# First layer of a two-layer graph network: gate products with one factor in PSUM, and the last bias added by a product with ones

## The chip, the cores and the metric

The kernel runs on one core of a Trainium2 chip. The metric is the device time of one execution, in microseconds (us), as the median of several runs. Engines are named as the profile names them: PE is the matrix engine (TensorE) and PEld its weight loads, DVE is VectorE, ACT is ScalarE, POOL is GpSimd, SP is SyncE, which here only issues DMAs. SBUF is the large on-chip memory; PSUM is the small one into which PE writes.

## The reference

There are 6250 nodes with 256 features, and 106250 edges sorted by target, among them one loop a node. The first layer runs a small network on the features at each edge's source (one of two, by the edge's kind), sums over a node's edges, and passes the sum through gates and three dense steps. The second layer is an attention layer. Both are added to their input and normalised.

```python
def layer0(feat, src, dst, rel, W_rel, b_rel, W_ih, b_ih, b_hh, W1, b1, W2, b2, W3, b3):
    S = feat[src]
    msgs = where(rel == r, relu(relu(S @ W_rel[r].T + b) @ W_rel[r].T + b), ...)   # r = 0, 1
    agg = segment_sum(msgs, dst)
    i, f, g, o = split(agg @ W_ih.T + b_ih + b_hh, 4, axis=-1)
    c = sigmoid(i) * tanh(g)
    hn = sigmoid(o) * tanh(c)
    x = relu(hn @ W1.T + b1)
    x = relu(x @ W2.T + b2)
    return x @ W3.T + b3

x = layernorm(x + layer0(x, src, dst, edge_type, ...))
x = layernorm(x + layer1(x, src, dst, ...))     # attention with 4 heads, softmax by target, layernorm, relu
```

## The kernel before

**Overall.** The messages depend only on the source node and the kind, so they are computed once for each node and kind and stored as a table in HBM (`parts0`). The first layer then gathers one row of that table an edge and sums the rows by target. The 100000 edges other than loops, sorted by target, are cut into 782 tiles of 128 edges. Fourteen tiles (two windows of seven) make a group, whose targets fill at most 128 node slots: there are 56 groups, numbered 0 to 55. The first layer ends with a table `rows1` in HBM, and the second layer gathers from it in the same way, tile by tile. A check takes this path, the function `fast`, when the edges are found sorted.

**The order.** Within `fast`, the order of each engine's instructions is the order in which the program writes them (`tc.manual_schedule()`): nothing is reordered afterwards, and an engine waits at its next instruction until its inputs and its buffer are there. The main loop of the first layer writes one gather (on POOL, an indirect DMA, L1367) and, four tiles behind it, one product of a one-hot matrix with the gathered rows (on PE, L1777, `sum0`). After each tile it calls `run.step()`, which goes through the chains that are under way. A chain is a Python generator; `yield n` means that its next piece is written n tiles later. After the last tile, `run.finish()` writes what is left of all chains, still in steps.

**The chains of the first layer.** `turn` takes a group's finished sum, adds the loops' share (L1549, twice) and transposes it (PE L1560, DVE copy L1563). `update` takes the groups together: four at a time up to group 47 (12 quads), then two pairs, and then groups 52 to 55 one by one, so 18 updates. An update with `cols` = 512, 256 or 128 columns goes through these steps, with pauses of `slow` tiles (3 early on, 1 in the last updates) between them:

1. for each half m = 0, 1: gates `gi`, `gg`, `go`, each of two products into one PSUM tile (L1627) and a sigmoid or tanh by ACT from there into SBUF (L1635); then `gg * gi` on DVE, in place, into the cell (L1640), written when all three gates of the half are written;
2. tanh of both cells on ACT, in place in SBUF (L1644), a pause, then tanh times `go` on DVE into `hn` (L1647), both halves together;
3. the product with W1 (L1651) and its relu (L1655), the product with W2 (L1658) and its relu (L1660);
4. right after that relu, `b3` added on DVE to the features `xn` of each group (L1663). `b3r` holds b3 in all 128 partitions, 256 numbers in each;
5. for each group, the product with W3 (L1672), the features added to it on DVE out of PSUM (L1674) and the statistics (L1676, L1677);
6. the square root on ACT (L1681), the reciprocal (L1683) and the normalisation (L1688) on DVE, transposes on PE (L1697), a copy by ACT (`fyT`, L1701), another bias (L1703);
7. the product with the second layer's weights (L1710), copies by ACT (L1716, L1717), stores of the rows by SP (L1723). The last group's rows are stored by an indirect DMA on POOL instead (L1725).

All products of `turn` and `update` share one ring of five PSUM tiles of a bank each (`fpg`). The sums have two further banks, and one bank holds constants of DVE and ACT (`bank`).

**The seam.** After the last tile of the first layer, POOL first issues 18 gathers of the second layer that depend only on rows stored by then (`gather_early`); then comes L1725, after it three more such gathers, and then the gathers of the second layer. Rows of the last three groups that such an early gather lacked are added later by PE (L1859).

Of the kernel before, what the change touches and what calls it, by code (L numbers as in the profile page):

```python
# [33 lines left out]
F32 = mybir.dt.float32  # L34
I32 = mybir.dt.int32
AF = mybir.ActivationFunctionType
# [6 lines left out]
P = 128  # L43
N = 6250
D = 256
# [662 lines left out]
def gnn_kernel(  # L708
# [572 lines left out]
    with tc.If(odd_v == 0) as cmp:  # L1281
        fast(
            tc, x, WihT, bih, bhh, W1T, b1, W2T, b2, W3T, b3, Wg, att_src, att_dst, bias, gamma,
            beta, out, parts0, rows1, slots, cuts, kept, iota_f, iota_p, ident, idx0, idx1,
            first, mark, slot, low_i, tail_i, tail_x, idx_e, own_n, srcs,
        )
# [8 lines left out]
def fast(  # L1295
# [40 lines left out]
    nc = tc.nc  # L1336

    def at(ap, offset, dims):
        return bass.AP(tensor=ap.tensor, offset=ap.offset + offset, ap=dims)

    def rows(ap, n):
        return at(ap, 0, [[0, P], [1, n]])
# [57 lines left out]
    everyone = slice(0, P)  # L1400
# [40 lines left out]
    def ring(pool, shape, dtype, name, n):  # L1441

        of = rings.setdefault((name, id(pool)), [[], 0])
        if len(of[0]) < n:
            of[0].append(pool.tile(shape, dtype, name=f"{name}_{len(of[0])}"))
        of[1] += 1
        return of[0][(of[1] - 1) % n]
# [19 lines left out]
    with (  # L1467
# [14 lines left out]
        W3T_s = l0w.tile([P, D], F32, name="fW3T")  # L1482
# [1 line left out]
        bh = l0w.tile([P, 8], F32, name="fbh")  # L1484
        b1c = l0w.tile([P, 1], F32, name="fb1c")
        b2c = l0w.tile([P, 1], F32, name="fb2c")
        b3r = l0w.tile([P, D], F32, name="fb3r")
        bias_r = l0w.tile([P, D], F32, name="fbias")
        with nc.allow_non_contiguous_dma(reason="bias vectors, one element a partition"):
            nc.sync.dma_start(bg, bih.rearrange("(m p) -> p m", p=P))  # L1490
            nc.sync.dma_start(bh, bhh.rearrange("(m p) -> p m", p=P))
            nc.sync.dma_start(b1c, b1.rearrange("(p o) -> p o", o=1))
            nc.sync.dma_start(b2c, b2.rearrange("(p o) -> p o", o=1))
        nc.sync.dma_start(b3r, rows(b3, D))
        nc.sync.dma_start(bias_r, rows(bias, D))
        nc.sync.dma_start(WihT_s, WihT.rearrange("(k p) f -> p k f", p=P))
        nc.sync.dma_start(W1T_s, W1T.rearrange("(k p) f -> p k f", p=P))
# [104 lines left out]
        def update(groups, aT):  # L1602
            slow = min(3, max(1, (NG - 4 - groups[0]) // 4))
            cols = len(groups) * P
            at_w = lows_of([w for g in groups for w in windows_of(g)])
            if groups == [NG - 1]:

                xn = [rows_x[NG - 1]]
                yield 2
            else:  # L1610
                xn = [ring(up, [P, D], F32, "fxn", 8) for g in groups]
# [3 lines left out]
            hn = ring(up, [P, 2, 4 * P], F32, "fhn", 2)  # L1615
            cells = []
            for m in range(2):
                gate = {}
                for name, part, func in (
                    ("gi", 0, AF.Sigmoid),  # L1620
                    ("gg", 2, AF.Tanh),
                    ("go", 3, AF.Sigmoid),
                ):
                    c = 2 * part + m
                    pg = ring(upp, [P, 4 * P], F32, "fpg", 5)
                    for k in range(2):
                        nc.tensor.matmul(  # L1627
                            pg[:, :cols],
                            WihT_s[:, k, c * P : (c + 1) * P],
                            aT[:, k, :cols],  # L1630
                            start=(k == 0),
                            stop=(k == 1),
                        )
                    gate[name] = ring(up, [P, 4 * P], F32, "f" + name, 2 if part == 0 else 4)
                    nc.scalar.activation(  # L1635
                        gate[name][:, :cols], pg[:, :cols], func, bias=bg[:, c : c + 1]
                    )
                    yield (slow + 1) // 2
                cell = gate["gg"][:, :cols]
                nc.vector.tensor_mul(cell, cell, gate["gi"][:, :cols])  # L1640
                cells.append((cell, gate["go"][:, :cols]))
            yield slow - 1
            for m, (cell, go) in enumerate(cells):
                nc.scalar.activation(cell, cell, AF.Tanh)  # L1644
            yield slow
            for m, (cell, go) in enumerate(cells):
                nc.vector.tensor_mul(hn[:, m, :cols], cell, go)  # L1647
            yield slow
            p1 = ring(upp, [P, 4 * P], F32, "fpg", 5)
            for k in range(2):  # L1650
# [7 lines left out]
            nc.tensor.matmul(p2[:, :cols], W2T_s, z1[:, :cols], start=True, stop=True)  # L1658
            z2 = ring(up, [P, 4 * P], F32, "fz", 3)
            nc.scalar.activation(z2[:, :cols], p2[:, :cols], AF.Relu, bias=b2c)  # L1660
            for i, g in enumerate(groups):
                u = everyone
                nc.vector.tensor_add(xn[i], xn[i], b3r)  # L1663
            yield slow
            mv = ring(up, [P, 4, 2], F32, "fmv", 3)
            rstd = ring(up, [P, 4], F32, "frstd", 3)
# [2 lines left out]
            for i, g in enumerate(groups):  # L1669
                u = everyone  # L1670
                p3 = ring(upp, [P, 4 * P], F32, "fpg", 5)[:, : 2 * P]
                nc.tensor.matmul(p3, z2[:, i * P : (i + 1) * P], W3T_s, start=True, stop=True)  # L1672
                y = keep3[i][u, 0, :]
                nc.vector.tensor_add(y, p3[u, :], xn[i])  # L1674
                st = ring(up, [P, nc.vector.BN_STATS_DIM], F32, "fst", 3)
                nc.vector.bn_stats(st[u, :], y)  # L1676
                nc.vector.bn_aggr(mv[u, i, :], st[u, :])  # L1677
                yield 1
# [6 lines left out]
            for i, g in enumerate(groups):  # L1685
                u = everyone
# [5 lines left out]
            for i, g in enumerate(groups):  # L1692
                u = everyone
# [12 lines left out]
            for i, g in enumerate(groups):  # L1706
                u = everyone
# [80 lines left out]
        for n in range(TC + LAG):  # L1788
            if n < TC:
                g, t = order[n]  # L1790
                k, turns = n % WT, n // WT // 10 % 2
                if k == 0:
# [3 lines left out]
                    m = min(WT, TC - n)  # L1796
# [15 lines left out]
            if n >= LAG:  # L1812
                g, t = order[n - LAG]
# [13 lines left out]
    with (  # L1827
# [285 lines left out]
        while t < TC + LAG or late or queue or run.chains:  # L2113
# [8 lines left out]
            if 0 <= k < TC:  # L2122
# [3 lines left out]
                g = w // 2  # L2126
# [87 lines left out]
```

## Time and profile before

| | |
|---|---|
| median of 3 runs | 2231.43 us (2231.18 to 2232.48) |
| profiled execution, its own time | 2231.32 us |
| its span | 2229.5 us |
| busy: PE, DVE, ACT, POOL | 1576.9, 1259.0, 506.4, 1527.2 us |
| the first layer's gathers | from 197 to 1186 us of the span |
| the second layer's gathers | from 1186 to 2178 us |

The span is the time between the first and the last record of the profile; 1.8 us of the execution's own time lie outside it. Times within the trace are us from the start of the span. A group of instructions is named by its line, engine and operation, what it writes and what it reads (buffer numbers left out), shapes as partitions x elements, and a count; behind the bar stand the busy time in us and the mean duration in ns, and behind a second bar the idle time of that engine before the group, with what ended it. In the timeline, the first two numbers of a line are start and duration, and the brackets at the end hold the engine's idle time ahead of it. A matmul of float32 numbers shows as two records.

### The profile page before, as it was taken

How to read it: one execution, taken by the hardware profiler on the slowest of the kernel's cores; microseconds unless marked ns; L12 is line 12 of the kernel's file. 1: busy time of each engine (PE TensorE's matmuls, PEld its weight loads, DVE VectorE, ACT ScalarE, POOL GpSimd, SP SyncE). 2: the span in 40 equal slices, each digit the busy share in tenths (PEclk: the TensorE clock that was granted, in tenths of full speed). 3: DMA queues.
4: the chain of work that ended last, by engine and by line, in shares of the span. 5: the costliest groups of instructions: out<-in, count | busy, mean ns of one | idle time of the engine just before them, and what ended most of it. 6: DMA issues, size and time to landing. Idle time of an engine off the chain costs nothing. (4 is left out here: it accounts for less than half of the span.)

```text
span 2229.5 us, 22334 instructions
## 1 busy us (share of the span) xinstructions
PE 1576.9 (71%) x5848; PEld 789.2 (35%) x5848; DVE 1259.0 (56%) x3374; ACT 506.4 (23%) x1526; POOL 1527.2 (68%) x1604
## 2 busy tenths in 40 slices
PE   8997788888888888888996754654545545454563
PEld 5664233333333333333453522322322223232331
DVE  7562134334333333333543688887777777777785
ACT  3332012221222212222343022212112111212121
POOL 1303777777777777777776777777777777777770
PEclk9998799899999899999997967766767677676776
DMA  5335435555455555554565556556555555555551
GB/s 165 131 103 155 130 114 172 165 153 149 147 171 165 146 151 155 170 168 134 178 175 162 150 145 165 156 145 165 148 153 156 144 159 143 164 155 145 156 151 38
DMA packets 163982, 334.33 MB, mean 150 GB/s; under 512 B 42538, under 2 KB 74398, under 8 KB 163845
## 3 DMA queue, kind: packets, MB, share of 16 engines
q0 software_dynamic: 75968, 208.00, 34.3%
q1 hardware_dynamic: 86085, 121.77, 17.3%
q10 hardware_dynamic: 1792, 3.05, 0.5%
q8 instruction: 48, 0.79, 0.1%
q14 instruction: 89, 0.73, 0.1%
HBM read 280.16 MB, written 52.53 MB: 149 GB/s over the span
## 5 line engine op out<-in xcount | busy, mean ns | idle before, releaser
L1367 POOL DMA_INDIRECT G<-parts,fidx x782 | 748.3, 957 | 330.5 <-issue 218.4
L1367 POOL DMA_INDIRECT G<-rows,fidx x761 | 727.4, 956 | 231.8 <-issue 214.2
L1777 PE MATMUL fps<-G,oh 128*64 128x257 f32 (+1 forms) x1674 | 528.1, 428 | 146.3 <-DMA G<-parts,fidx 129.5
L2101 PE MATMUL fps<-gw,oh 128*64 128x264 f32 (+1 forms) x1674 | 433.7, 463 | 246.3 <-DVE gw L1992 246.1
L2101 PEld LDWEIGHTS fps<-gw,oh 128*64 128x64 f32 (+1 forms) x1674 | 222.7, 164 | 411.9 <-DVE gw L1992 266.0
L1777 PEld LDWEIGHTS fps<-G,oh 128*64 128x64 f32 (+1 forms) x1674 | 193.6, 148 | 454.7 <-DMA G<-parts,fidx 237.2
L1992 DVE TENSOR_TENSOR gw<-G,bank 128x1792 f32<-128x1792 f32 (+1 forms) x167 | 248.9, 1490 | 62.4 <-ACT gw L1991 60.4
L1545 DVE TENSOR_SCALAR kind<-fps 128x1 f32<-128x1 f32 x112 | 12.5, 153 | 315.0 <-PE fps L1777 315.0
L1627 PE MATMUL fpg<-faT,fWihT 128*128 128x512 f32 (+2 forms) x432 | 170.9, 519 | 0.2 <-DVE faT L1563 0.2
L1452 DVE TENSOR_TENSOR oh<-bank,fslot 128x1024 f32<-128x1024 f32 x112 | 136.1, 1215 | 7.2 <-ACT bank L1971 7.2
L1940 PE MATMUL turn<-fident,e 128*120 128x128 f32 (+2 forms) x30 | 12.3, 412 | 155.3 <-ACT e L2136 155.3
L1242 PE MATMUL fpm<-fWrT,fhT 128*128 128x256 f32 x392 | 92.9, 392 | 5.3 <-DVE fms L1250 5.3
L1627 PEld LDWEIGHTS fpg<-faT,fWihT 128*128 128x128 f32 x432 | 70.9, 190 | 69.1 <-issue 59.4
L1738 DVE COPY nd<-hr 128x4 f32<-128x4 f32 x53 | 10.1, 190 | 149.7 <-ACT hr L1716 149.7
L1228 PE MATMUL fph<-fxc,fWrT 128*128 128x512 f32 (+1 forms) x208 | 88.8, 579 | 4.7 <-DMA fWrT<-in_WrT_dram 4.7
L2047 ACT ACTIVATE fy<-fy,frs 128x256 f32<-128x256 f32 x112 | 66.8, 596 | 86.9 <-DVE frs L2044 39.4
L2041 ACT ACTIVATE frs<-fmv,eps_c 128x1 f32<-128x1 f32 x112 | 32.9, 294 | 235.7 <-DVE gw L1986 152.7
L1242 PEld LDWEIGHTS fpm<-fWrT,fhT 128*128 128x128 f32 x392 | 75.6, 196 | 24.3 <-DVE fms L1250 9.1
L1710 PE MATMUL fpg<-Wx,fyT 128*128 128x264 f32 x224 | 74.2, 460 | 3.0 <-ACT fyT L1701 3.0
L944 POOL DMA_INDIRECT packed<-frame,place x21 | 20.9, 995 | 76.7 <-DVE frame L909 70.6
L1250 DVE TENSOR_TENSOR fms<-fpm,fbrr 128x512 f32<-128x512 f32 x49 | 33.6, 688 | 68.7 <-PE fpm L1242 62.8
L2144 ACT COPY e<-G 128x28 f32<-128x28 f32 x112 | 23.8, 213 | 183.8 <-DMA G<-rows,fidx 147.2
(253 smaller groups left out, 1863.4 us busy)
## 6 DMA issues: line engine op xcount, KB each, us to landing
kept<-keep SPq DMA_DIRECT2D x56, 384.0 KB
k<-kept SPq DMA_DIRECT2D x56, 384.0 KB
dB<-slots SPq DMA_DIRECT2D x112, 128.0 KB
loop<-parts SPq DMA_DIRECT2D x110, 128.0 KB
parts<-fms SPq DMA_DIRECT2D x49, 256.0 KB
G<-parts,fidx POOLq DMA_INDIRECT x782
G<-rows,fidx POOLq DMA_INDIRECT x761
fxn<-in_x_dram SPq DMA_DIRECT2D x110, 64.0 KB
```

Source lines behind the costliest of these rows:

```text
L1228: nc.tensor.matmul(ph[:, :cols], WrT_s[:, r, k, m * P : (m + 1) * P], xc[:, k, :cols], start=(k == 0), stop=(k == 1),)
L1242: made = nc.tensor.matmul(pm[:, r, :], hT[:, r, k, j * P : (j + 1) * P], WrT_s[:, r, k, :], start=(k == 0), stop=(k == 1),)
L1250: nc.vector.tensor_add(ms.rearrange("p r f -> p (r f)"), pm.rearrange("p r f -> p (r f)"), brr)
L1367: return nc.gpsimd.indirect_dma_start(out=to_tile, out_offset=None, in_=table, in_offset=bass.IndirectOffsetOnAxis(ap=idx, axis=0),)
L1452: nc.vector.tensor_tensor(to[:, :nj, :], iota_s[:, None, :].to_broadcast([P, nj, SLOTS]), of[:, :, None].to_broadcast([P, nj, SLOTS]), op= ...
L1627: nc.tensor.matmul(pg[:, :cols], WihT_s[:, k, c * P : (c + 1) * P], aT[:, k, :cols], start=(k == 0), stop=(k == 1),)
L1710: nc.tensor.matmul(ph[u, :], hs[i][:, k, u], Wx[:, k, :], start=(k == 0), stop=(k == 1))
L1777: nc.tensor.matmul(sums[g][to, :], ohj, got[t], start=begins, stop=ends)
L1992: nc.vector.tensor_mul(gw[:, :, :D].rearrange("p j (h f) -> p j h f", h=H), of[:, :n, :D].rearrange("p j (h f) -> p j h f", h=H), ex[:, o ...
L2041: nc.scalar.activation(r, mv[u, k, 1:2], AF.Ln, bias=eps_c[u])
L2047: nc.scalar.activation(y, y, AF.Identity, bias=m, scale=r)
L2101: nc.tensor.matmul(sums[g][to, :], ohj, gw, start=begins, stop=ends)
```

## The change

Three things change in `update`. In the gate `gg`, the tanh is written back into the PSUM tile from which it was read, and the cell is computed on DVE from that tile and `gi` right after it, ahead of the gate `go`. The tanh of the cell is written into a further PSUM tile of the ring `fpg`, and the product with `go` reads it there; the two halves now follow each other with a pause of `(slow + 1) // 2` tiles after each tanh, where before both tanh and then both products were written with a pause of `slow` between. And `b3` is no longer added to the features on DVE: a second product, of a row of 128 ones with the row b3, adds it to the PSUM sum of W3. For it `b3r` becomes one row, loaded by a smaller DMA, and a memset on DVE fills the row of ones.

```diff
-        b3r = l0w.tile([P, D], F32, name="fb3r")
+        b3r = l0w.tile([1, D], F32, name="fb3r")
+        one_r = l0w.tile([1, P], F32, name="one_r")
+        nc.vector.memset(one_r, 1.0)
...
-        nc.sync.dma_start(b3r, rows(b3, D))
+        nc.sync.dma_start(b3r, at(b3, 0, [[0, 1], [1, D]]))
...
-                    gate[name] = ring(up, [P, 4 * P], F32, "f" + name, 2 if part == 0 else 4)
+
+                    gate[name] = (
+                        pg
+                        if name == "gg"
+                        else ring(up, [P, 4 * P], F32, "f" + name, 2 if part == 0 else 4)
+                    )
                     nc.scalar.activation(
                         gate[name][:, :cols], pg[:, :cols], func, bias=bg[:, c : c + 1]
                     )
+                    if name == "gg":
+                        cell = ring(up, [P, 4 * P], F32, "fgg", 4)[:, :cols]
+                        nc.vector.tensor_mul(cell, pg[:, :cols], gate["gi"][:, :cols])
                     yield (slow + 1) // 2
-                cell = gate["gg"][:, :cols]
-                nc.vector.tensor_mul(cell, cell, gate["gi"][:, :cols])
                 cells.append((cell, gate["go"][:, :cols]))
             yield slow - 1
             for m, (cell, go) in enumerate(cells):
-                nc.scalar.activation(cell, cell, AF.Tanh)
-            yield slow
-            for m, (cell, go) in enumerate(cells):
-                nc.vector.tensor_mul(hn[:, m, :cols], cell, go)
+                pc = ring(upp, [P, 4 * P], F32, "fpg", 5)[:, :cols]
+                nc.scalar.activation(pc, cell, AF.Tanh)
+                yield (slow + 1) // 2
+                nc.vector.tensor_mul(hn[:, m, :cols], pc, go)
             yield slow
...
-            for i, g in enumerate(groups):
-                u = everyone
-                nc.vector.tensor_add(xn[i], xn[i], b3r)
             yield slow
...
-                nc.tensor.matmul(p3, z2[:, i * P : (i + 1) * P], W3T_s, start=True, stop=True)
+                nc.tensor.matmul(p3, z2[:, i * P : (i + 1) * P], W3T_s, start=True, stop=False)
+                nc.tensor.matmul(p3, one_r, b3r, start=False, stop=True)
```

## The prediction

> **What bounds the kernel now.** I read the page's busy times and slices first.
>
> ```profile
> PE 1576.9 (71%) x5848; PEld 789.2 (35%) x5848; DVE 1259.0 (56%) x3374; ACT 506.4 (23%) x1526; POOL 1527.2 (68%) x1604
> ...
> PE   8997788888888888888996754654545545454563
> ...
> POOL 1303777777777777777776777777777777777770
> ```
>
> By busy time PE leads, but its share falls by half in the second layer while nothing else slows. POOL stands at 7 from slice 5 to slice 39, but for one 6 in slice 22, where the two layers meet (1170 to 1226 us). Why 7 and not 9, the waits of POOL tell (who waited for what: total us, times, longest), and then its group of the first layer's gathers:
>
> ```profile
> POOL G L1367 <- issue: 437.4, 1436, 0.3
> POOL G L1367 <- ACT G L1798: 92.5, 1, 92.5
> ...
> POOL rows L1725 <- ACT keep L1717: 5.4, 1, 5.4
> ```
>
> ```profile
> L1367 POOL DMA_INDIRECT G<-parts,fidx x782 | 748.3, 957 | 330.5 <-issue 218.4 <-ACT G L1798 92.5 <-PE fps L1777 5.2
> ```
>
> A gather takes about 0.95 us and the next follows 0.30 us after its end, waiting for nothing: a chain of 1.25 us a tile. The 92.5 us are before the first gather. From 197 to 2178 us the only real wait is the 5.4 us at the seam, where L1725 needs the last group's rows. So the time is POOL's: work on PE, ACT or DVE counts only where it makes a gather longer or lengthens that seam.
>
> Some gathers are longer. The timeline of all engines around 565 us shows why:
>
> ```profile
> 565.44 0.69 DVE L1640 TENSOR_TENSOR fgg<-fgg,fgi 128x512 f32<-128x512 f32 x1 [2.64 <-ACT fgg L1635]
> 565.50 1.45 POOL L1367 DMA_INDIRECT G<-parts,fidx  x1 [0.30 <-issue]
> ...
> 567.25 0.94 POOL L1367 DMA_INDIRECT G<-parts,fidx  x1 [0.30 <-PE fpg L1627]
> ```
>
> L1640, with both factors in SBUF, began just ahead of the gather and ended at 566.13. The gather took 0.50 us more than 0.95, and the next began 1.75 us after it instead of 1.25. I went through all gathers from 197 to 1213 us: each lengthened one (over 0.02 us) but the first has a DVE instruction across its start, and its excess is that instruction's end less the gather's start less 0.13 us (here 0.63 - 0.13). By line: L1647 3.24 us (11 gathers), L1640 2.47 us (11), L1663 1.33 us (15), L1549 1.26 us, L1703 0.52 us, L1688 0.27 us; with the first gather's own 0.04 and traces, 9.2 us in all. The groups of DVE, shapes apart, in the same stretch:
>
> ```profile
> L1452 DVE TENSOR_TENSOR oh<-bank,fslot 128x1024 f32<-128x1024 f32 x56 | 67.8, 1211 | 0.0
> ...
> L1674 DVE TENSOR_TENSOR keep<-fpg,fxn 128x256 f32<-128x256 f32 x56 | 23.8, 424 | 30.4 <-PE fpg L1672 28.1
> ...
> L1663 DVE TENSOR_TENSOR fxn<-fxn,fb3r 128x256 f32<-128x256 f32 x56 | 20.2, 417 | 0.0
> L1640 DVE TENSOR_TENSOR fgg<-fgg,fgi 128x512 f32<-128x512 f32 x24 | 16.6, 692 | 41.9 <-ACT fgg L1635 39.3 <-issue 2.6
> L1647 DVE TENSOR_TENSOR fhn<-fgg,fgo 128x512 f32<-128x512 f32 x24 | 16.4, 687 | 3.4 <-ACT fgg L1644 2.4
> ```
>
> The first two rows are the control: one factor lies in PSUM (`bank`, `fpg`). L1452 covers a gather's start 53 times and L1674 8 times, and not one of those gathers is lengthened.
>
> [...]
>
> **The change, part by part.**
>
> *Stalls removed.* After the change L1640's product reads a PSUM tile and `gi`, L1647's a PSUM tile and `go`; L1663 is gone. By the control none can hold a gather: 2.47 + 3.24 + 1.33 = 7.04 us. Of this 0.21 us fall on early gathers after 1186 us, which end in a wait anyway. **Gain 6.8 us.** Bounds: L1549, L1703 and L1688 stay, with 2.05 us now. Their starts shift with the order; an instruction of length L at a random phase costs about (L - 0.13)² / 2.5 on average, 0.05 us for 0.48 us, so 56 of L1549's second form and 56 of L1703 and L1688 each could cost near 7 us. They follow PE and ACT, which follow the gathers, so I keep 2 us: -1 to +2 us.
>
> *DVE and ACT work.* 56 additions of 0.417 us (23 us) go; DVE is busy about a third of this stage, hence nothing. The products move from SBUF to PSUM: L1674 (PSUM, 424 ns) against L1663 (SBUF, 417) gives 7 ns each. ACT's work keeps its count. Memset and smaller DMA come around 200 us, ahead of no gather: nothing, within 0.2 us.
>
> *The product with ones.* 56 more products of 256 columns, two records each. L1672 is the nearest row (39.7 us for 112 records, 0.71 us a product); fewer rows need not make it faster, so 0.35 to 0.9 us. PE gains 40 us in a stage of 990 us in which it is busy 848 us. Its idle time, mostly waiting for gathered rows, hides them, except near the seam. POOL runs up to 70 tiles ahead of PE before the ring of gathered tiles stops it.
>
> *The ring `fpg`.* Two more tiles an update, and `gg`'s tile is held until DVE has read it. A tile is taken again five allocations later, over a tile's time away: nothing, up to 1 us at the seam.
>
> *Steps moved.* From the W1 product on, an update is written one tile (1.25 us) later, its row stores on SP and the stores of `kept` behind them too. The early gathers need group 52's stores; SP issued these by 1170 us and the first such gather comes at 1186: 16 us of cover. The cell's product, earlier on DVE, waits there for `gg` from ACT, as before (39.3 us idle ahead of L1640); behind it wait one-hots and sums' tails that PE has 70 tiles for. Nothing, 0 to 0.5 us.
>
> *The seam.* Here the cover is gone: L1725 waits for the last group's chain, and 5.35 us of it stand out behind the early gathers. The timelines of POOL, of ACT and of PE there:
>
> ```profile
> 1207.69 0.95 POOL L1367 DMA_INDIRECT G<-rows,idx_e  x1 [0.30 <-issue]
> 1213.99 1.00 POOL L1725 DMA_INDIRECT rows<-rows_l,tail_i  x1 [5.35 <-ACT keep L1717]
> ```
>
> ```profile
> 1197.31 1.28 ACT L1681 ACT_TABLE_LOAD   x1
> ...
> 1198.92 1.28 ACT L1635 ACT_TABLE_LOAD   x1
> ...
> 1200.60 1.28 ACT L1635 ACT_TABLE_LOAD   x1
> ```
>
> ```profile
> 1176.03 2.28 PE L1777 MATMUL fps<-G,oh 128*128 128x257 f32 x4 [3.33 <-DMA G<-parts,fidx]
> ```
>
> At 1176 PE last waits for rows; from there to the last group's sum (1191.4) it works without a gap, so what is added there delays the chain. I followed the yields by hand. The one-by-one updates need four steps where they had three, so group 53's W2 product (0.49 us) moves behind that wait, and its product with ones (0.71) is new: +1.2 us. After the last sum, group 54's W1 product comes behind a gate of group 55, and its ones product delays the later gates: about +1.4 us. Group 54's square root moves from between `gi` and `gg` of the second half to between `gg` and `go`: tanh no longer needs a load of its own, one of the three loads goes, -1.3 us. Group 55's own ones product: +0.7 us. Sum **+2.0 us**, bounds -0.5 (PE has slack) to +4 us (each step waits). Behind L1725 queue the last three early gathers and the whole second layer, so this counts in full.
>
> *Sum:* -6.8 + 2.0 = -4.8 us. The profiled execution's 2231.32 us (span 2229.5) becomes 2226.5; the median stands 0.1 us above it: **2226.6 us**.
>
> **Rivals.**
>
> 1. *Slower: PE becomes the bound before the seam.* From 1080 to 1190 us PE is idle only 8 us, 3.3 of them at 1176, and ten ones products (7 us) fall there. If the granted clock, at 0.93 to 1.0 there, drops by a tenth, PE's last 110 us last 11 us longer and the seam's stall grows from 5.35 to about 17 us: +11.5 - 6.8 = +4.7, 2236 us. It decides from a growth of the stall over 6.8 us; measurable slowing needs 11.3. Against it: PE caught up three times after 1150 us.
> 2. *The collisions move.* L1549, L1703 and L1688 fall on gathers near the random rate: +4 us, 2230.6 us. For it: every step after the gates shifts. Against it: the same offsets recur in quad after quad today.
> 3. *A free seam.* PE's idle time takes the products and the dropped table load shows: -0.7 us there, 2224 us.
> 4. *The change doesn't do what it says:* the stall comes from the write or from `gi` alone; no gain, +2.0, 2233.4 us. Against it: 61 controls.
>
> **How the numbers follow.** Main case 0.55, rivals 0.10, 0.15, 0.17, 0.03. A measurement here can tell about 0.2%, 4.5 us, so "faster" means under 2227.0. The main case (2223.5 to 2229.5) lies there in some 6 of 10, 0.34; rival 3 adds its 0.17: faster 0.51. Slower is rival 1 with its higher half and little else: 0.10. Same 0.39. Range: the gain with a free seam and 1 us fewer collisions, 2222.8, to all but the worst of rival 2, 2231.0.
>
> **What would show it.** Gathers of 1.0 us and more under the gate products gone, the first layer's last gather near 1179 instead of 1186 us, L1452 and L1549 unchanged; two table loads, not three, in the last updates; a wait of some 7 us ahead of L1725. It is wrong if gathers are still lengthened under products with a PSUM factor, or if the wait ahead of L1725 passes 10 us.

## The result and the profile after

In runs of both kernels side by side the kernel after takes 2228.02 us (median; 2226.2 to 2233.2) and the kernel before 2233.26 us: a ratio of **0.9979, 95% interval 0.9971 to 0.9987**. In a second set of runs the medians are 2224.25 and 2228.55 us, the ratio 0.9982 (0.9975 to 0.9990). So the change is worth 4.3 to 5.2 us, against a forecast of 4.8. (The 2226.6 us of the forecast were reckoned from 2231.4 us; in the first of these sets the kernel before took 1.8 us more than that.)

Busy time and slices of the kernel after:

```profile
PE 1601.2 (72%) x5960; PEld 805.4 (36%) x5960; DVE 1235.8 (56%) x3319; ACT 504.7 (23%) x1526; POOL 1523.6 (68%) x1604
...
PE   8997789888888889989996754554555545455563
...
POOL 1303777777777777777776777777777777777770
```

PE gained 24 us net in its records, DVE lost 23, and slice 22 of POOL is still a 6. The waits of POOL (total us, times, longest), and its group of the first layer's gathers:

```profile
POOL G L1367 <- ACT G L1804: 90.8, 1, 90.8
```

```profile
POOL rows L1731 <- ACT keep L1723: 4.8, 1, 4.8
```

```profile
L1367 POOL DMA_INDIRECT G<-parts,fidx x782 | 744.2, 952 | 328.9 <-issue 216.4
```

The same three lines as before, little changed: the waits are 90.8 and 4.8 us where they were 92.5 and 5.4, and the mean gather of the first layer is 952 ns instead of 957. The groups of DVE in that stage, shapes apart (lines have moved: L1640 is now L1647, L1647 is L1655, L1674 is L1680):

```profile
L1452 DVE TENSOR_TENSOR oh<-bank,fslot 128x1024 f32<-128x1024 f32 x56 | 67.8, 1210 | 0.0
...
L1680 DVE TENSOR_TENSOR keep<-fpg,fxn 128x256 f32<-128x256 f32 x56 | 23.8, 425 | 73.1 <-PE fpg L1678 71.7 <-DMA loop<-parts 1.4
...
L1647 DVE TENSOR_TENSOR fgg<-fpg,fgi 128x512 f32<-128x512 f32 x24 | 16.6, 692 | 106.2 <-ACT fpg L1642 106.2
L1655 DVE TENSOR_TENSOR fhn<-fpg,fgo 128x512 f32<-128x512 f32 x24 | 15.3, 681 | 1.3 <-ACT fpg L1653 1.3
```

The gate products last as long as they did (692 and 681 ns), but one factor is now `fpg`, and **not one gather is lengthened under them any more**. The excess (what the gathers take over 0.95 us each, added up as in the prediction, here up to the last gather of the first layer) fell from 8.8 to 2.8 us; what is left is L1551 (the former L1549) 1.8 us, L1709 (L1703) 0.6, L1694 (L1688) 0.3. That is 6.0 us; in a second profiled execution of the kernel after it is 2.0, a fall of 6.8.

The seam is best read as three stretches. "Sum" is the start of L1545 (now L1547) on the last group, the first instruction that reads its sum:

| us | first to last gather of layer 1 | last gather to sum | sum to tail store | first gather to tail store |
|---|---|---|---|---|
| before | 987.8 | 6.7 | 22.6 | 1017.1 |
| after | 983.8 | 5.4 | 23.2 | 1012.3 |
| after, second profile | 980.9 | 8.7 | 23.8 | 1013.3 |

The tail store is L1725 (now L1731). From the first gather to it both profiles of the kernel after have about the forecast's gain (-4.8 and -3.8 us), divided up differently. From the tail store to the end, where no code was changed, the three profiles take 1015.6, 1017.8 and 1013.0 us: single executions scatter there by about as much as the change is worth.

The first two profiles can't be compared gather by gather without one more reading. The median distance from one gather to the next is 1251 ns before and 1254 ns after, in both layers, stalls or none. Over the 782 gathers of the first layer that is some 2 us against the kernel after: of the 6.0 us of stalls saved there, 4.0 are left in the first column. So the exact 4.8 us of this profile are in part chance. The experiments below show that the spacing is not a property of this kernel.

### The profile page after: what moved, and what is told of

The parts are those of the page before. It is cut to its first block, busy times and chain, and to the rows that moved or that the text cites. A ratio compares the mean times of both kernels' runs of the same rounds, so it can differ in the third digit from the quotient of the medians.

```text
span 2225.4 us, 22485 instructions
## 1 busy us (share of the span) xinstructions
PE 1601.2 (72%) x5960; PEld 805.4 (36%) x5960; DVE 1235.8 (56%) x3319; ACT 504.7 (23%) x1526; POOL 1523.6 (68%) x1604
## 3 DMA queue, kind: packets, MB, share of 16 engines
q1 hardware_dynamic: 85943, 121.64, 17.6%
## 5 line engine op out<-in xcount | busy, mean ns | idle before, releaser
L1783 PE MATMUL fps<-G,oh 128*64 128x257 f32 (+1 forms) x1674 | 510.9, 426 | 120.1 <-DMA G<-parts,fidx 100.1
L1547 DVE TENSOR_SCALAR kind<-fps 128x1 f32<-128x1 f32 x112 | 12.4, 152 | 177.5 <-PE fps L1783 177.5
L1647 DVE TENSOR_TENSOR fgg<-fpg,fgi 128x512 f32<-128x512 f32 (+2 forms) x36 | 20.6, 573 | 143.2 <-ACT fpg L1642 143.2
L1565 DVE COPY faT<-fpg 128x256 f32<-128x256 f32 x56 | 23.8, 425 | 97.5 <-PE fpg L1562 95.8
L1716 PE MATMUL fpg<-Wx,fyT 128*128 128x264 f32 x224 | 76.6, 472 | 1.3 <-ACT fyT L1707 1.3
```

What stands on the lines that cost most here:

```text
L1565: nc.vector.tensor_copy(aT[:, :, i * P : (i + 1) * P], pt.rearrange("p (k n) -> p k n", k=2))
L1716: nc.tensor.matmul(ph[u, :], hs[i][:, k, u], Wx[:, k, :], start=(k == 0), stop=(k == 1))
L1783: nc.tensor.matmul(sums[g][to, :], ohj, got[t], start=begins, stop=ends)
```

## The experiments

The first four (of the fourth, its first run) ran on a chip where the kernel before itself takes 3078 us. POOL waits there for other engines, in experiment 1's profile 526 us for L1992 on DVE in the second layer (2.7 us in the kernel before as profiled above), and PE's mean granted clock is 0.72 instead of 0.83; why was not found. Of those four I use how long gathers were. Their times are given, but the ratios follow neither the stalls nor the products with ones: experiments 1 and 3 both have these products, and stand at 1.0083 and 0.9987.

The "port theory" of three expectations is a name only, for what the first of them puts in brackets: that a product with both factors in SBUF holds up a gather that starts under it. By what means it does so no run shows.

**1. One part alone: b3 by a product with ones, gates as before** (edit against the kernel before).

```diff
-                nc.vector.tensor_add(xn[i], xn[i], b3r)
...
+                nc.tensor.matmul(p3, one_r, b3r, start=False, stop=True)
```

> The kernel before with only the last part of the change: b3 added by the product with ones, no addition on VectorE; the gate products stay in SBUF. Port theory (a product with both factors in SBUF holds up a gather that starts under it; placement alone decides): the first layer's gathers lose only the share of the additions, their excess over 0.95 us falls from 8.8 to about 7.5 us (6.5 to 8.5), all of it under L1640, L1647 and L1549. Seam: if the products with ones lengthen the chain as predicted, from the last gathered tile to the tail store 29.3 us become 30.7 (29.3 + 0.7 for group 53 + 0.7 for group 55); if keeping the matrix engine busy saves it the slow clock after its wait, they become 28 or less. Time: -1 us by the port theory with a long seam, -3 with a short one. Rival (load theory: fewer VectorE instructions in all are what helps): excess falls by the share of VectorE time removed, 20 of about 360 us, so by 0.5 us.

Measured: excess 7.35 us, 5.3 of it under the two gate products, none under the addition that is gone. Ratio 1.0083 (1.0053 to 1.0113), where a gain of 1 to 3 us had been expected. The stalls of the gates don't depend on b3's path.

**2. The other part alone: gates in PSUM, b3 on VectorE** (edit against the kernel after).

```diff
+                nc.vector.tensor_add(xn[i], xn[i], b3r)
...
-                nc.tensor.matmul(p3, one_r, b3r, start=False, stop=True)
```

> The changed kernel with b3 added on VectorE again and no product with ones; only the gate products have a factor in PSUM. Port theory: excess of the first layer's gathers 2.8 + 1.3 = about 4 us (3.2 to 5.5), none of it under the two gate products, about 1.3 us under the addition of b3. Load theory: VectorE has the same work as before, so excess near 8.8 us. Seam: with no product with ones the matrix engine should wait before the seam and run slowly after it, as in the kernel before: 29 us or more from the last gathered tile to the tail store; if the product with ones only costs, 27.5 us. Time against before: -4.5 us by the port theory, 0 by the load theory.

Measured: excess 4.08 us, none under the gate products, 1.6 under b3's addition; ratio 0.9967 (0.9950 to 0.9983).

**3. The order of the change without PSUM.** Here the products come in the new places and with the new pauses, but both factors lie in SBUF (edit against the kernel after).

```diff
-                    gate[name] = (pg if name == "gg" else ring(...))
+                    gate[name] = ring(up, [P, 4 * P], F32, "f" + name, 2 if part == 0 else 4)
...
-                        nc.vector.tensor_mul(cell, pg[:, :cols], gate["gi"][:, :cols])
+                        nc.vector.tensor_mul(cell, cell, gate["gi"][:, :cols])
...
-                pc = ring(upp, [P, 4 * P], F32, "fpg", 5)[:, :cols]
+                pc = cell
```

> The changed kernel in its order, instruction for instruction, but with both factors of the gate products in SBUF again (tanh of the gate and of the cell written to SBUF, in place in the cell). Port theory: the gathers under these two products are held up again, excess 2.8 + about 5.7 = 8.5 us (5 to 11, as their phase against the gathers is another one), each excess equal to the product's end less the gather's start less 0.13 us. Order theory (the gain comes from writing the products at other places, or in two halves): excess stays near 2.8 us and the time equals that of the changed kernel. Time against before: 0 to +2 us less the share of b3, so about -1 (port), -4.7 (order).

Measured: ratio 0.9987 (0.9970 to 1.0005); excess 11.5 us, 8.7 of it under the gate products: somewhat above the upper end of the range, and four times what a theory of order allows. **So the place of one factor decides, not the order and not DVE's load.** With the control of 1 and 2 this is shown, not argued.

**4. A product of zeros added to the kernel before.**

```diff
-                nc.tensor.matmul(p3, z2[:, i * P : (i + 1) * P], W3T_s, start=True, stop=True)
+                nc.tensor.matmul(p3, z2[:, i * P : (i + 1) * P], W3T_s, start=True, stop=False)
+                nc.tensor.matmul(p3, toward[0:1, 1, :], b3r[0:1, :], start=False, stop=True)
```

> The kernel before with one more product of a single row added to each sum of W3, a row of zeros as weights, so that nothing is added to the sum: the matrix engine's work of the change without its other parts. Excess of the gathers: 8.8 us, unchanged within 1.5 us. Cost theory (as predicted: each product with ones in the seam's chain counts): from the last gathered tile to the tail store 29.3 becomes 30.7 us, time +1.4 us. Clock theory (the matrix engine waited 3.3 us at 1172 to 1176 us and then ran at half clock for 4 us; more work there keeps it from waiting): 27.5 to 28.5 us, no wait over 2 us before the seam, granted clock 1.00 in the ten us after it, time -1 us.

Measured on the first chip: excess 8.8 us, unchanged; ratio 1.0057 (1.0036 to 1.0078); the seam, with a wait of 32 us there, told nothing. It was run again where the kernel before takes 2227.4 us:

> The kernel before with one product of a row of zeros added to every output product of the first layer: 56 times 2 products become two, some 0.71 us each, and nothing else changes (the row of toward that it uses is zero by construction, b3 is still added on VectorE). Clock theory of the last groups: the 3.3 us that PE waited for rows and the half clock after it are filled, and from the last gather of the first layer to the tail store it takes 27.5 to 28.5 us instead of 29.3; the excess of the gathers stays at 8.8 us, so the time falls by about 1 us (0 to 2). Cost theory, as predicted: the product of the last group lies on the path, 29.9 to 30.9 us, and the time rises by 0.5 to 1.5 us. PE as bound: a wait over 6 us ahead of the tail store and a time 5 us or more longer.

Measured: 2229.23 us, ratio 1.0006 (0.9998 to 1.0014), 1.9 us above the kernel before and so a little more than the cost theory's 1.5; excess 8.1 us; 30.75 us from the last gather to the tail store: the cost theory's number, but not by its way. The last gather to the sum takes 5.6 us, 1.1 less than before in spite of the added products, as the clock theory has it (no wait for rows after 1051 us, and a granted clock of 1.00 from there to the sum); from the sum to the tail store it takes 25.2 instead of 22.6. There the two products of zeros on the path show, and one of them runs at half speed:

```profile
1190.89 0.69 PE L1673 MATMUL fpg<-fb3r,toward 1*128 1x256 f32 x2
...
1203.11 1.22 PE L1672 MATMUL fpg<-fW3T,fz 128*128 128x256 f32 x2 [0.46 <-ACT fz L1660]
1204.27 1.22 PE L1673 MATMUL fpg<-fb3r,toward 1*128 1x256 f32 x2
```

The first takes 0.62 us from start to start, the second 1.22. With what the half-speed W3 product takes more (1.22 against 0.70 us before) that is 2.4 of the 2.6 us. Neither theory alone was right.

**5. The kernel after again, beside the gates alone.** The second profiled execution and the second set of times told of above:

> The kernel after, unchanged, a second profiled execution beside the other kernels of this set. If the median period of the gathers (1254 ns in its first profile, 1251 in that of the kernel before) belongs to the kernel, it is 1254 again and the time stays where it was; if it is a matter of the single execution, it can be 1251, and the span is then 4 us shorter. Excess of the first layer's gathers 2.8 us again; 28.5 us from the last gather to the tail store if the full clock of the first profile is the kernel's, 29.5 or more if it was the execution's. Ratio to the kernel before 0.997 to 0.9987.

Measured: gathers 1251 ns apart. So the 1254 don't belong to the kernel (experiment 8's kernel, too, shows 1251 in one profile and 1254 in the next, though on another chip). The chip alone does not decide it either: on the chip of the first experiments, experiment 2 shows 1251 and the other three 1254. The excess is 2.0 us and the gathers' stretch 7.0 us shorter than before: **the gain of 6.8 us is there in full**. But the tail store starts 1013.3 us after the first gather, no earlier than in the first profile, although the last gather started 3 us sooner: the seam took 32.5 us, not 28.5. The gates alone on the same chip:

> The kernel after with b3 added to the features on VectorE as in the kernel before (no product with ones): the PSUM part of the change alone. By the prediction's steps the stalls under the gate products go (5.7 us), those under the addition of b3 stay (1.1 to 1.6 us), and the ones products' 1.4 us at the end are saved: ratio 0.9965 to 0.998, within 0.1% of the kernel after. If the ones products cost more than their own place at the end (PE late over the whole layer), gates alone is faster than the kernel after by over 2 us (ratio 0.9955 to 0.997).

Measured: 2222.91 us, ratio 0.9971 (0.9961 to 0.9982), in the mean 1.3 us below the kernel after (95% interval 0.2 to 2.3), less than the 2 us that the second theory asked for; excess 4.1 us, of which 2.1 under b3's addition. The change's second part takes 2.1 us of stalls away and is still no gain: in the profiles the tail store comes 1012.8 us after the first gather with the gates alone, and 1013.3 in the kernel after beside it. When PE last waited for gathered rows points to the reason (timelines of PE: gates alone, then the kernel after in both profiles):

```profile
1169.53 1.49 PE L1783 MATMUL fps<-G,oh 128*128 128x257 f32 x4 [3.11 <-DMA G<-parts,fidx]
```

```profile
1043.24 0.62 PE L1783 MATMUL fps<-G,oh 128*64 128x257 f32 x2 [0.34 <-DMA G<-parts,fidx]
```

```profile
1040.22 3.23 PE L1783 MATMUL fps<-G,oh 128*64 128x257 f32 x6 [1.28 <-DMA G<-parts,fidx]
```

In the kernel before this was 1176 us, as the prediction showed. With the ones products PE catches up with the gathers for the last time at 1040 to 1043 us and then runs behind them for 140 us to the sum. From there on a shorter gather no longer brings the sum forward. The products of zeros alone do the same to the kernel before: in experiment 4's second run PE last waited for rows at 1050 us.

**6. Four products where the change has one.** Three more products of zeros an output, all after the ones product, with no effect on the sums:

```diff
-                nc.tensor.matmul(p3, one_r, b3r, start=False, stop=True)
+                nc.tensor.matmul(p3, one_r, b3r, start=False, stop=False)
+                for more in range(3):
+                    nc.tensor.matmul(p3, toward[0:1, 1, :], b3r, start=False, stop=(more == 2))
```

> The kernel after with three more products of a row of zeros for every output product, all adding nothing to the sums: TensorE gets 168 products in two parts, 0.71 us each, some 120 us more. TensorE as the coming bound (rival 1): its waits in the first layer are used up, the ring of gathered rows fills, POOL waits, and the wait ahead of the tail store and before it adds up to 15 to 35 us, time 10 to 30 us above the kernel after. If TensorE has room: only the seam's share, 3 times 0.7 to 1.4 us, 2 to 6 us.

Measured: 2263.02 us, ratio 1.0155 (1.0141 to 1.0168), 38.8 us above the kernel after: PE as bound, and past my upper end. The gathers' excess is 1.6 us, so it is not they; POOL waits in two places (timeline of POOL):

```profile
1184.77 0.95 POOL L1367 DMA_INDIRECT loop<-parts,tail_x  x1 [24.18 <-DVE agg L1551]
...
1244.46 1.00 POOL L1733 DMA_INDIRECT rows<-rows_l,tail_i  x1 [17.56 <-ACT keep L1725]
```

24.2 us ahead of the last group's loop rows, whose tile is free only when an earlier group is through, and 17.6 at the tail store. The rows of the two kinds of products, and busy time and clock by stage (the column after POOL's is PE's granted clock):

```profile
L1680 PE MATMUL fpg<-fb3r,toward 1*128 1x256 f32 x336 | 129.0, 540 | 0.0
...
L1678 PE MATMUL fpg<-fb3r,one_r 1*128 1x256 f32 x112 | 55.0, 582 | 0.0
```

```profile
200.00:600.00 400.00, 373.10 (x1149) 175.35 (x1150) 122.83 (x379) 72.90 (x180) 302.63 (x320) 0.85 0.54 155
600.00:1000.00 400.00, 393.83 (x1264) 194.56 (x1263) 141.31 (x473) 92.42 (x242) 302.75 (x320) 0.87 0.55 158
1000.00:1170.00 170.00, 168.91 (x543) 88.95 (x541) 58.87 (x201) 41.27 (x109) 121.61 (x129) 0.83 0.54 156
```

```profile
200.00:600.00 400.00, 343.09 (x1056) 139.68 (x1056) 127.22 (x390) 73.29 (x182) 302.76 (x319) 0.90 0.53 154
600.00:1000.00 400.00, 351.45 (x1122) 147.95 (x1121) 138.67 (x464) 92.14 (x240) 302.95 (x319) 0.94 0.55 160
1000.00:1170.00 170.00, 160.78 (x586) 79.19 (x585) 69.66 (x249) 58.12 (x149) 128.71 (x135) 0.96 0.56 163
```

The second fence is the kernel after. 129 us of products were added. PE's busy time from 1000 to 1170 us was 160.8 of 170 already; with more of it (168.9) the granted clock was 0.83 there instead of 0.96, the same products took longer (the ones product 582 ns a record instead of 436), and the rest came out at the end. PE had not paused before it slowed: it has no wait from 1100 to 1142 us, and in that time a ones product takes 0.69 us at 1121.89 and the next 1.22 at 1125.87; without a wait again, 0.69 at 1159.50 and 1.22 at 1163.55. I had not put a falling clock into this expectation.

**7. More factors in PSUM.** In `turn` the first addition writes back into the sums, so the second has a factor there; in the second layer the sum, its scaling and an addition do the same.

```diff
-            for r, of in ((0, ps[:, :D]), (1, agg)):
-                nc.vector.scalar_tensor_tensor(agg, loop0[g][...], kind[:, r : r + 1], of, ...)
+            for r, to in ((0, ps[:, :D]), (1, agg)):
+                nc.vector.scalar_tensor_tensor(to, loop0[g][...], kind[:, r : r + 1], ps[:, :D], ...)
...
-            nc.vector.tensor_add(y, y, ps[u, :D])
-            read.add(g)
+            nc.vector.tensor_add(ps[u, :D], y, ps[u, :D])
...
-            nc.vector.tensor_mul(heads(y), heads(y), den...)
-            nc.vector.tensor_add(y, y, k3[u, 1, :])
+            nc.vector.tensor_mul(heads(ps[u, :D]), heads(ps[u, :D]), den...)
+            nc.vector.tensor_add(y, ps[u, :D], k3[u, 1, :])
+            read.add(g)
```

> The kernel after, in which three more operations of VectorE get one factor in PSUM: the first of the two additions of the loop rows in turn writes its result back over the sums in PSUM, so the second reads it there, and in the second layer's finish the sum, its scaling by 1/den and the addition of k3 keep their running value in PSUM, the sums being given free after the last of them. Placement theory: of the excess of the first layer's gathers the 1.8 us under the loop addition go, 1.0 stay; of the second layer's 6.6 us the 1.6 and 0.4 under the scaling and the addition go; with 7 ns for each operand in PSUM hidden, the time falls by 3 to 4 us against the kernel after, about 8 us against the kernel before (ratio 0.996 to 0.9975). Rival, the sums held longer delay PE: gathers of the second layer are unchanged but PE's wait for the free sums grows, and the time stays within 1 us of the kernel after (ratio 0.9975 to 0.999) or rises.

Measured: the first layer's excess is 0.6 us, nothing under the loop addition. Yet the ratio is 0.9986 (0.9979 to 0.9992), no better than the kernel after's 0.9982 on another chip. The last gather to the sum takes 8.4 us. This is the rival's ratio, though for another reason than it named: PE is behind since 1039 us, as in the kernel after since 1040. From there to the sum PE was without work for 4.2 us, in the kernel after's second profile for 3.8, and from the tail store to the end it takes 1014.4 us, where the kernel after takes 1017.8 and 1013.0. So no cost of the sums held longer shows.

**8. The same without the ones product**, b3 being added to the third product where it lies in PSUM:

```diff
-                nc.tensor.matmul(p3, one_r, b3r, start=False, stop=True)
+                nc.vector.tensor_add(p3, p3, b3r)
```

> The kernel e7 (loop rows and the second layer's sum kept in PSUM as well) with the ones product taken out and b3 added on VectorE to the third product in PSUM, so that this addition has one factor in PSUM: 112 products of some 0.36 us each leave TensorE, 56 additions of 0.42 us return to VectorE. If TensorE is late by then (e7 took 8.3 us from the last gather to the end of the last group's sum where the kernel after took 5.3), that stretch is 5.3 to 7 us here and the time 2 to 4 us below e7's 2223.9 (ratio to the kernel before 0.9965 to 0.998); if TensorE is not late, it is within 1 us of e7 (0.998 to 0.999). Excess of the first layer's gathers 0.6 us in both cases.

Measured: 2221.58 us, ratio 0.9966 (0.9953 to 0.9978), in the mean 3.0 us below the kernel after beside it (95% interval 1.3 to 4.7). The excess is 1.3 us, not 0.6, nearly all of it under L1692 and L1707 (formerly L1688 and L1703) and none under b3's addition. The last gather to the sum takes 7.5 us, though: a little over the expected end, and in this profile PE last waited for rows at 1042 us even so. Its clock is low there (a mean of 0.66 from 1040 to 1050 us, and 0.83 from 1140 to 1150; behind the wait, four records of L1714 take 2.13 us at 1044.58, and 1.16 at 1051.70), which may be why; no run tests it. Run again on another chip:

> The kernel e8, unchanged, once more: ratio to the kernel before 0.9955 to 0.9978, and first gather to tail store 1010 to 1011.5 us again, with 30 to 31.5 us from the last gather of the first layer to the tail store. If its lead over the kernel after was chance, the ratio is 0.998 to 0.999.

Measured: 2222.20 us beside 2231.03 for the kernel before, ratio 0.9958 (0.9944 to 0.9971). Excess 1.7 us. First gather to tail store 1010.8 and 1010.1 us in the two. In the second, with gathers 1254 ns apart, PE waits for rows up to 1174 us and the seam takes 27.6 us, less than expected. The addition of b3, and the tail store of that profile:

```profile
L1676 DVE TENSOR_TENSOR fpg<-fpg,fb3r 128x256 f32<-128x256 f32 x56 | 23.6, 422 | 33.1 <-PE fpg L1675 33.0
```

```profile
1203.91 1.00 POOL L1729 DMA_INDIRECT rows<-rows_l,tail_i  x1 [4.14 <-ACT keep L1721]
```

422 ns an addition where the product took 0.71 us of PE, and a wait of 4.1 us ahead of the tail store instead of the 8.8 of the kernel after's second profile. This version beats the kernel before in two sets, and the kernel after in the one set where both ran.

**9. The change with only its second part done so** (the edit of experiment 8, on the kernel after).

> The kernel after with only its second part done otherwise: the ones product is taken out, and b3 is added on VectorE to the third product where it lies in PSUM, so that the addition has one factor in PSUM and one in SBUF. 112 products (40 us) leave TensorE, 56 additions of 0.42 us return to VectorE; no gather should wait under the addition (2.1 us in the kernel with the gates alone). Theory, TensorE is late at the end of the first layer and the ones products are a part of that: first gather to tail store 1010.5 to 1012, time 1 to 2.5 us below the kernel after (ratio to the kernel before 0.9965 to 0.9978). Rival, the wait is only moved: what TensorE saves, the addition on VectorE gives back at the end, and the time is that of the kernel after within 0.7 us (0.9978 to 0.9985).

Measured: 2225.15 us beside 2231.03, ratio 0.9969 (0.9957 to 0.9981); excess 2.6 us, none under b3's addition; sum to tail store 22.1 us, the shortest of all. The ratio lies within the first theory's range, but first gather to tail store is 1012.1 us, just outside that range and hardly less than the kernel after's 1012.3, and the intervals of the ratios overlap. Whether this alone beats the change is not settled. But PE again waits for rows late, at 1169 us. So without the added products it does so between 1169 and 1176 us in four profiles of five (experiment 8's first is the fifth; the slow chip is left aside), and with them in none.

## Why the prediction was right

*Stalls removed, 6.8 us.* Right. Excess 8.8 us before, 2.8 and 2.0 after; the two profiles with gathers 1251 ns apart differ by 7.0 us from the first gather to the last. Experiments 1 to 3 show the cause. The remaining stalls of L1549, L1703 and L1688, kept at 2 us, came to 2.6 and 1.9 us: rival 2 (collisions move) did not happen.

*DVE and ACT work, and the ring, at nothing.* Nothing in the runs contradicts it: the distance of the gathers follows their own duration and stalls, and no wait for a tile of `fpg` stands out. The 7 ns for a PSUM operand were not even needed: the products lasted 692 and 681 ns, where they had taken 692 and 687.

*Steps moved, at 0 to 0.5 us.* Not quite. Among what queues on DVE behind the cell's product the prediction named one-hots and sums' tails, but the normalisation of another update can queue there too. At 1144 us the cell's product of group 52 waits for its tanh, which on ACT comes after a square root and a table load of 1.28 us; the normalisation of the second pair waits behind that product on DVE, and PE waits for the normalisation (timeline of PE, kernel after):

```profile
1145.85 0.44 PE L1703 MATMUL fpg<-fident,keep 128*128 128x128 f32 x2 [1.73 <-DVE keep L1694]
```

Of the profiles with the change's order, those of the slow chip left aside, all but experiment 6's show this wait (1.55 to 1.73 us, at 1141 to 1146); the kernel before and experiment 4's second run don't. Where PE has caught up by the end it costs nothing; where PE is behind since 1043 us it adds to its delay. How much of the time it is worth no run separates.

*The product with ones, 0.71 us each.* Right in size (group of PE):

```profile
L1678 PE MATMUL fpg<-fb3r,one_r 1*128 1x256 f32 x112 | 39.9, 436 | 0.0
```

One row cost as much as 128: 39.9 us for 112 records, where the W3 product (L1677) took 40.2 for as many. **Wrong was how far idle time hides it**: "its idle time hides them, except near the seam". Idle time does so up to 1043 us; in the last 140 us there is none to take them.

*The seam, +2.0 us.* In size about right: the bounds were -0.5 to +4, measured were -0.7 in the first profile, just outside, and +3.2 in the second. The term that failed is the +1.2 us ahead of the sum, which rested on the last wait for rows at 1176 us. That wait no longer exists. The term measured -1.3 in the first profile and +2.0 in the second. The gathers' pace alone does not explain the difference: from the first gather, the last wait for rows ends after 848.0 us in the first profile and after 846.1 in the second, for the same tile, so the shorter gathers did bring it forward by 2 us. Then the same 534 records of PE to the sum took 141.2 us at a mean granted clock of 1.00 in the first, and 143.5 at 0.98 in the second, where the clock was 0.50 from 1041 to 1047 us, right behind the last wait (1.28 us; four records of L1716 took 2.13 us at 1043.38, and 1.16 at 1050.46). So the sum came 989.2 and 989.5 us after the first gather although the last gathers lie 3 us apart. That the two come so close is chance, as far as is known.

That -1.3 was possible because the kernel before paid for its wait twice. Its stages around the last wait (busy time by engine, the column after POOL's is PE's granted clock):

```profile
1172.00:1176.00 4.00, 0.69 (x4) 0.30 (x2) 1.16 (x4) 1.84 (x4) 2.86 (x4) 0.94 0.78 237
1176.00:1180.00 4.00, 3.97 (x9) 1.95 (x10) 0.47 (x2) 0.00 (x0) 3.09 (x4) 0.50 0.33 98
1180.00:1184.00 4.00, 4.00 (x15) 2.01 (x14) 1.87 (x6) 1.00 (x2) 3.09 (x4) 0.70 0.38 111
```

After 3.3 us without work PE ran at 0.50 of its clock for 4 us and at 0.70 for 4 more; the four records of L1777 that the prediction showed took 2.28 us where the same four took 1.18 at full clock 20 us earlier. In steps of 2 us the clock was 0.50 three times from 1176 to 1182 us and then 0.91, with PE busy for 7.97 of these 8 us. The kernel after has 1.00 over the same stretch, in which its PE waits for no rows. By what rule the clock falls no run shows. But the trace of the kernel before had the fall, and the prediction should have used it, both for the wait that goes and for products behind short waits at the end of the chain (there, behind waits of 1.9 and 2.5 us, the clock was 0.61 from 1202 to 1206 us).

*The terms after the sum, +1.4, +0.7 and -1.3 us.* Right: together +0.8, measured +0.6 and +1.2. The dropped table load shows in the timeline of ACT:

```profile
1192.03 1.28 ACT L1687 ACT_TABLE_LOAD   x1
...
1193.63 1.28 ACT L1642 ACT_TABLE_LOAD   x1
...
1200.05 1.28 ACT L1687 ACT_TABLE_LOAD   x1
```

Before, 1197.31, 1198.92 and 1200.60 were three in a row for one square root, with a fourth at 1207.12; now there are two, and then the last group's. It goes with the order of the two functions: before, the tanh came first after the square root, and the sigmoid behind it had a load of its own (1200.60); now the sigmoid comes first (its load at 1193.63), and the tanh at 1195.45 has none. (With the sigmoid first, one load served both elsewhere too: in the kernel before, six gates and two tanh follow the load at 1121.68, and the next is the square root's at 1139.17.) But the layer has as many loads as before, 37: the one dropped here turns up among the gates of group 52, where 1141.53, 1143.14 and 1144.80 now stand three in a row, with the tanh (1144.44) ahead of the sigmoid (1146.09). The wait ahead of L1731 was to be some 7 us: 4.8 and 8.8.

*The rivals.* Rival 3's -0.7 us at the seam is what the first profile shows, but the second shows +3.2, so the seam is not free. Rival 1, PE as the bound, is half true: since 1043 us PE does set the end of the stage, but the wait at the tail store grew from 5.4 to 8.8 us at most, by half of the 6.8 us that would have used up the gain. Experiment 6 shows its edge, falling clock included.

**What stays open.** Why the gathers are 1251 ns apart in one execution and 1254 in another was not found. The second layer's differences are not explained beyond it: its gathers' excess was 7.7, 6.6 and 5.1 us in the three profiles, under instructions that no one touched, and the stretch after its last gather 52.4, 54.1 and 52.7 us. And how much of PE's delay in the last 140 us is the products with ones, how much the moved steps and how much the clock, is argued from single profiles.

## What to carry to other kernels

Where indirect gathers follow one another without a wait (here 0.30 us after the one before), look for DVE instructions with two SBUF factors across their starts, and put one factor into PSUM: here 5.7 us of stalls under two products came to none. By the trace of the kernel before, one such instruction cost a gather at most its own length less 0.13 us, and moving it elsewhere in the order is luck: from experiment 1 to experiment 3, on one chip, the stalls under the gate products rose from 5.3 to 8.7 us by the new order alone. When moving such an operation to another engine instead, ask from which time on that engine will run behind, not how much idle time it has in all: in the kernel before PE was busy 91% of the time from 1000 to 1170 us, and it was the next bound. An addition with one PSUM factor on DVE (0.42 us) looks cheaper than a one-row product on PE (0.71): experiment 8 speaks for it, and experiment 9, where nothing else was changed, does not settle it. Before a step moves ahead of others on an engine, list everything that then queues behind its wait. And compare single executions only stage by stage: here the same kernel's stages differed by 3 us, which hid and showed the bound in turn.

## What the runs showed of the hardware

A product of a single row lasted as long as one of 128 rows (39.9 and 40.2 us for 56 products each in the kernel after, 0.71 and 0.72 us for 256 columns of float32). With PE busy for 935.8 us in experiment 6 and 855.3 in the kernel after, from 200 to 1170 us, its mean granted clock over the whole execution was 0.794 and 0.828; in experiment 6 a ones product took 1.22 us instead of 0.69 at 1126 us, while PE worked without a wait. And in the kernel before PE lost about as much again behind a wait of 3.3 us: 4 us at 0.50 and 4 us at 0.70 of the clock are 2.0 and 1.2 us. An indirect gather on POOL was lengthened by a DVE instruction with two SBUF factors across its start, in the first layer by 8.8 us in all, and with one factor of three such operations moved to PSUM and the fourth gone (experiment 7) by 0.6.
